# Two of three additions in each sum of features: from GpSimd instructions to accumulating transfers

## The chip, the core and the metric

The kernel runs on one core of a Trainium2 chip. The metric is the device time of one execution in microseconds; smaller is better. A core has TensorE (PE in the profile) for matrix products, VectorE (DVE), ScalarE (ACT) and GpSimd (POOL) for elementwise work, and SyncE (SP), which here issues the transfers. Sixteen DMA engines carry out transfers for all of them.

## What is computed

The reference is a mixture of eight gated experts plus one shared expert, all of them applied to every token, added to the input:

```
g = einsum('bsd,edf->ebsf', h, Wg)
u = einsum('bsd,edf->ebsf', h, Wu)
expert_outs = einsum('ebsf,efd->ebsd', silu(g) * u, Wd)
expert_output = einsum('be,ebsd->bsd', gating_probs, expert_outs)
shared = einsum('bsf,fd->bsd', silu(h @ Sg) * (h @ Su), Sd)
return x + (1 - sg) * expert_output + sg * shared
```

`x` has 8 batch rows of 512 tokens with 256 channels, in 32-bit floats. There are 8 experts with 1024 hidden features each, and the shared one is treated as a ninth.

## The kernel before, in words

**Tiling.** The work is cut into 36 units: 2 halves of the batch (4 batch rows each), 9 experts, and 2 groups of 512 hidden features. In a unit there are four slices of 128 hidden features, numbered by i, and four batch rows, numbered by j. The unit needs the 16 products of slice i with batch row j, once for the gate (m = 0) and once for the up projection (m = 1), then 16 tiles of features h[i,j] = silu(gate) x up x gating weight (`finish`, L449 to L460; 128 features by 512 tokens each, 256 KB), and then their product with the down weights, summed over slices and experts.

**Fewer products.** The products are not all made directly. The four diagonal ones (i = j) are made from the two halves of the 256 channels (`P_step` L463, `Q_step` L487), and the twelve others come in six pairs (`PAIRS`, L65: (1,0), (0,2), (3,0), (1,2), (3,1), (3,2)) from sums and differences of inputs and of weights, with three matmuls for each pair and m (`R1_step` L508, `R_step` L518). Tiles named v, b are such forms of the inputs, loaded by SP; u, wb, at are forms of the weights, made by GpSimd (L380 to L406) with some help of ScalarE (L402). The down projection uses the same device (`down`, L562): besides three matmuls per pair with forms ud, wd of the down weights (`d_forms`, L427) it needs, for each slice n, the row sum rows[n] = h[n,0] + h[n,1] + h[n,2] + h[n,3] over the four batch rows, and for each batch row n the column sum cols[n] over the four slices.

**The sums.** Each of the eight sums of a unit takes three additions, 24 in all. After the last feature tile of a pair is made, `h_sums` (L530) appends four entries to the list `u.sums`: for pair (i,j) a row and a column addition of h[i,j], then a row and a column addition of h[j,i]. `add_sum` (L542) takes the list's first entry and issues its addition on GpSimd (L548). The first addition of a sum opens a tile (pool `sum`, 8 buffers) and writes h[n,n] plus the other feature tile into it; the second and third add one more feature tile to it in place. So over the list, the entries numbered from 1, the sums come in this order: rows 1, cols 0, rows 0, cols 1, rows 0, cols 2, rows 2, cols 0, rows 3, cols 0, rows 0, cols 3, rows 1, cols 2, rows 2, cols 1, rows 3, cols 1, rows 1, cols 3, rows 3, cols 2, rows 2, cols 3. In the last unit only the first three pairs are treated so (12 additions).

**The order of the work.** TensorE's and GpSimd's instruction orders are written by hand (`HAND`, L833; ScalarE's too in the first unit): each engine runs its instructions in program order, and waits on other engines where data are needed. The strings `HUB`, `BLOCK`, `ORDER`, `FIRST`, `LAST` (L808 to L814) interleave steps G of a unit's gate and up products (`gate_up`, L734) with steps D of the down projection of the unit before (`down`). The sums of a unit are issued beside steps G: one at every second step once the unit's own steps are past 22 (`TAKE`), and the rest at each step of the next unit until step 22 (L881 to L887). `down` reads the sums after pairs 0 to 4 in the order p0, q0, pair 5, q1, p1, q2, p2, q3, p3 (L644), where "p n" is the matmul with rows[n] (in `carried`, L596, shown as b<-rows,wd at L591) and "q n" that with cols[n] (in `single`, L604, shown as q<-cols,ad or q<-cols,wd at L607). Before each of them `flush_sums` (L550) issues what additions of that sum are still in the list.

**Buffers around it.** Feature tiles h rotate through 11 buffers (L80), sums through 8 (L81), b and wb through 2 each (L77), v through 3 (L76). A buffer is written again only after all its readers are done; the framework puts in the waits. SP issues the loads of v (L300), b (L317), w (L364) and wd (L411) in program order as their buffers come free. Before the change GpSimd issues no transfers.

Of the kernel before, what the change touches and what calls it, by code (L numbers as in the profile page):

```python
# [11 lines left out]
ALU = mybir.AluOpType  # L12
# [4 lines left out]
def kernel(  # L17
# [79 lines left out]
    gp = nc.gpsimd  # L97
# [246 lines left out]
    for h in range(NH):  # L344
        for e in range(NE):
            for g in range(GRP):
                u = Unit()
# [194 lines left out]
    def add_sum(u):  # L542
        which, n, at = u.sums.pop(0)
        sums = getattr(u, which)
        first = n not in sums
        if first:
            sums[n] = sumpool.tile([P, S], F32, tag="sum", name=f"{which}{n}_{u.name}")
        gp.tensor_tensor(sums[n], u.h_[n, n] if first else sums[n], u.h_[at], ALU.add)  # L548

    def flush_sums(u, which, n):  # L550
        while any(w == which and k == n for w, k, _ in u.sums):
            add_sum(u)
# [304 lines left out]
    for u in units:  # L857
# [6 lines left out]
        for what in FIRST if u.n == 0 else LAST if nxt is None else ORDER:  # L864
            if what == "G":
# [15 lines left out]
                if nG > TAKE and nG % 2 == 0 or nxt is None:  # L881
                    for _ in range(2 if nxt is None else 1):
                        if u.sums:
                            add_sum(u)
                for _ in range(2 if u.n and units[u.n - 1].opens else 1):
                    if nG < TAKE and u.n and units[u.n - 1].sums:
                        add_sum(units[u.n - 1])  # L887
# [69 lines left out]
```

## Time and profile before

| What | Value |
|---|---|
| Runs | 2445.86, 2445.99, 2448.1 us (median 2445.99) |
| Profiled execution, first to last instruction (span) | 2444.9 us, 22752 instructions |
| What lies around the span | 1.1 us to the runs' median; the page gives no other time for the execution |
| One unit of work | 66.95 us |
| Matmul of 128x512, start to start | 0.43 us |
| Addition of a sum on GpSimd, median | 1.27 us |
| DMA, mean share of the 16 engines, queue of SP | 34.3% |
| Granted TensorE clock | 1.00 |

How to read the profile: "busy" lines give each engine's busy time, its share of the span, and its instruction count. The "chain" follows the work that ended last backwards, from each instruction to what released it. A group line has source line, engine, operation, output<-inputs, shapes and count, then total busy time and mean time of one in ns, then idle time of the engine before such instructions, with what ended most of it. A timeline line has start, duration, engine, source line, operation, names and count, and in brackets the idle time before it and its releaser. A window line has the stretch, its length, the busy time of PE, weight loads, DVE, ACT and POOL, then the clock, the DMA share and GB/s. A DMA issue line ends with KB each and the median time from issue to landing in us.

### The profile page before, as it was taken

The numbers are of one execution on the slowest core, as the hardware profiler recorded it, in microseconds if no ns is written. First come the engines' busy times: TensorE is split into PE (matmuls) and PEld (weight loads), VectorE is DVE, ScalarE is ACT, GpSimd is POOL, SyncE is SP. The second block draws the span as 40 slices with busy tenths as digits, with TensorE's granted clock in tenths as the row PEclk, the third lists the DMA queues.
The fourth block names the chain that finished last, engine by engine and source line by source line (L and its number), as shares of the span: only waits on it lengthen the run. The fifth ranks groups of instructions, "written<-read, shape, count | busy, mean of one in ns | idle before, by whom it ended". The sixth has DMA issues, their size and how long they took to land.

```text
span 2444.9 us, 22752 instructions
## 1 busy us (share of the span) xinstructions
PE 2431.5 (99%) x5722; PEld 1079.6 (44%) x5722; DVE 1937.4 (79%) x2889; ACT 1247.2 (51%) x2308; POOL 2095.8 (86%) x2335
## 2 busy tenths in 40 slices
PE   9999999999999999999999999999999999999998
PEld 4444444444444444444444444444444444444444
DVE  7777878777777777787997777777877777777787
ACT  4555554554555555545455555555455455555543
POOL 7988888898988989898888888888888888888883
PEclk9999999999999999999999999999999999999999
DMA  4333333343333333344353222322333333232322
GB/s 160 99 104 112 101 113 114 103 134 100 128 108 97 106 111 95 106 131 126 112 138 119 92 84 90 96 84 88 100 103 103 104 95 95 84 95 89 95 91 82
DMA packets 219793, 255.82 MB, mean 105 GB/s; under 512 B 63632, under 2 KB 156048, under 8 KB 219664
## 3 DMA queue, kind: packets, MB, share of 16 engines
q1 hardware_dynamic: 219376, 254.34, 34.3%
q8 instruction: 48, 0.79, 0.1%
q14 instruction: 81, 0.66, 0.1%
q10 hardware_dynamic: 288, 0.04, 0.0%
HBM read 238.59 MB, written 15.73 MB: 104 GB/s over the span
## 4 chain that ended last, share of the span: by engine, by line
PE 96%; DVE 1%; POOL 1%; DMA 0%; issue 0%; ACT 0%; SPq 0%; DVEq 0%; ACTq 0%; POOLq 0%
PE c L521 30%; PE c L511 15%; PE c L489 10%; PE c L466 10%; PE r L607 7%; PE r L630 7%; PE S L591 5%; PE b L591 5%; PE q L607 5%; PE s L607 2%; PE tail L715 0%; DVE h L457 0%; POOL wd L437 0%; DMA sgt<-ondB_sharedgateprob_dram 0%; DVE accb L582 0%
## 5 line engine op out<-in xcount | busy, mean ns | idle before, releaser
L521 PE MATMUL c<-b,wb 128*128 128x512 f32 x1728 | 847.5, 592 | 0.0
L452 ACT ACTIVATE sg<-c 128x512 f32<-128x512 f32 x576 | 343.8, 597 | 587.2 <-DVE c L526 343.6
L457 DVE SCALAR_TENSOR_TENSOR h<-sg,coef,c 128x512 f32<-128x512 f32 x576 | 427.8, 743 | 235.1 <-PE c L521 132.4
L521 PEld LDWEIGHTS c<-b,wb 128*128 128x128 f32 x1728 | 327.9, 190 | 412.4 <-issue 389.8
L511 PE MATMUL c<-v,u 128*128 128x512 f32 x864 | 441.6, 593 | 1.2 <-ACT c L506 1.2
L548 POOL TENSOR_TENSOR rows<-rows,h 128x512 f32<-128x512 f32 x282 | 372.4, 1321 | 0.0
L548 POOL TENSOR_TENSOR cols<-cols,h 128x512 f32<-128x512 f32 x282 | 361.0, 1280 | 0.0
L516 DVE TENSOR_TENSOR c<-D,c 128x512 f32<-128x512 f32 x432 | 298.9, 692 | 77.8 <-ACT sg L452 57.9
L526 DVE TENSOR_TENSOR c<-c,D 128x512 f32<-128x512 f32 x432 | 298.6, 691 | 18.7 <-PE c L521 18.5
L466 PE MATMUL c<-x,w 128*128 128x512 f32 x572 | 274.5, 592 | 0.0
L404 POOL TENSOR_TENSOR wb<-u,wb 128x256 f32<-128x256 f32 x108 | 79.0, 732 | 222.4 <-ACT wb L402 222.4
L511 PEld LDWEIGHTS c<-v,u 128*128 128x128 f32 x864 | 163.4, 190 | 209.2 <-issue 167.4
L607 PE MATMUL r<-h,wd 128*128 128x512 f32 x426 | 217.5, 592 | 0.0
L630 PE MATMUL r<-X,ud 128*128 128x512 f32 x426 | 217.5, 592 | 0.0
L537 DVE TENSOR_TENSOR X<-h,h 128x512 f32<-128x512 f32 x213 | 208.4, 978 | 6.9
L489 PE MATMUL c<-x,at 128*128 128x512 f32 x432 | 209.6, 593 | 2.4 <-DVE P L482 2.2
L499 ACT COPY D<-c 128x512 f32<-128x512 f32 x284 | 165.9, 584 | 86.8 <-DVE h L457 86.8
L548 POOL TENSOR_TENSOR rows<-h,h 128x512 f32<-128x512 f32 x144 | 199.5, 1385 | 0.0
L548 POOL TENSOR_TENSOR cols<-h,h 128x512 f32<-128x512 f32 x144 | 186.4, 1294 | 0.0
L472 ACT COPY P<-c 128x512 f32<-128x512 f32 x216 | 126.6, 587 | 107.0 <-PE c L466 102.5
L466 PEld LDWEIGHTS c<-x,w 128*128 128x128 f32 x572 | 108.5, 190 | 135.8 <-issue 111.4
L590 ACT COPY S<-accS 128x512 f32<-128x512 f32 x135 | 79.6, 590 | 152.7 <-DVE accV L578 144.9
(110 smaller groups left out, 3478.4 us busy)
## 6 DMA issues: line engine op xcount, KB each, us to landing
b<-xs SPq DMA_DIRECT2D x210, 512.0 KB, 3.6
v<-xs SPq DMA_DIRECT2D x210, 256.0 KB, 2.6
w<-in_L_cond_Wg_dram SPq DMA_DIRECT2D x128, 128.0 KB, 3.4
w<-in_L_cond_Wu_dram SPq DMA_DIRECT2D x128, 128.0 KB, 3.5
wd<-in_L_cond_Wd_dram SPq DMA_DIRECT2D x32, 512.0 KB, 5.0
f<-xd SPq DMA_DIRECT2D x12, 512.0 KB, 3.3
xs<-f SPq DMA_DIRECT2D x18, 256.0 KB, 3.0
xin<-in_x_dram SPq DMA_DIRECT2D x16, 256.0 KB, 4.0
```

The lines of the kernel that those rows point to most:

```text
L452: nc.scalar.activation(s, bank, AF.Silu)
L457: ve.scalar_tensor_tensor(t, u.sg[i, j], coef[:, u.e, b : b + 1], bank, ALU.mult, ALU.mult)
L466: nc.tensor.matmul(bank, u.raw[i][:, m, 0], xhub[u.h, i][:, 0], start=True, stop=True)
L489: nc.tensor.matmul(bank, u.at[i][:, m], xhub[u.h, i][:, 1], start=False, stop=True, skip_group_check=True,)
L511: nc.tensor.matmul(bank, u.U[p][:, m], u.V[p], start=False, stop=True, skip_group_check=True)
L516: ve.tensor_sub(other, u.Ds[j, m], bank)
L521: nc.tensor.matmul(bank, u.W[p][:, r, m], u.VB[p][:, r], start=False, stop=True, skip_group_check=True,)
L526: ve.tensor_add(bank, bank, u.Ds[j, m])
L548: gp.tensor_tensor(sums[n], u.h_[n, n] if first else sums[n], u.h_[at], ALU.add)
L591: nc.tensor.matmul(po, w, b, start=not full, stop=True, skip_group_check=full)
L607: nc.tensor.matmul(po, w, b, start=True, stop=True)
L630: nc.tensor.matmul(A, u.Ud[p], u.X[p], start=False, stop=True, skip_group_check=True)
```

## The change

In `add_sum` the first addition of a sum stays a GpSimd instruction. The second and third become transfers that GpSimd issues, with the feature tile as source and the sum tile as destination, and with an accumulate: each element that arrives is added to what is there. List, order, tiles and buffers are the same.

```diff
         first = n not in sums
         if first:
             sums[n] = sumpool.tile([P, S], F32, tag="sum", name=f"{which}{n}_{u.name}")
-        gp.tensor_tensor(sums[n], u.h_[n, n] if first else sums[n], u.h_[at], ALU.add)
+        if first:
+            gp.tensor_tensor(sums[n], u.h_[n, n], u.h_[at], ALU.add)
+        else:
+            gp.dma_start(sums[n], u.h_[at], accum_op=ALU.add)
```

## The prediction

> **What bounds the kernel now.** I read the engines' busy shares first, then the chain that ended last.
>
> ```profile
> PE 2431.5 (99%) x5722; PEld 1079.6 (44%) x5722; DVE 1937.4 (79%) x2889; ACT 1247.2 (51%) x2308; POOL 2095.8 (86%) x2335
> ...
> PE 96%; DVE 1%; POOL 1%; DMA 0%; issue 0%; ACT 0%; SPq 0%; DVEq 0%; ACTq 0%; POOLq 0%
> ```
>
> TensorE sets the end: it holds 96% of the chain. A busy share is an average, so I then asked for busy time by stretch, with PE's first.
>
> ```profile
> 100.00:1200.00 1100.00, 1099.40 (x2561) 485.81 (x2560) 873.46 (x1300) 566.50 (x1048) 967.05 (x1069) 1.00 0.37 112
> 1200.00:2350.00 1150.00, 1148.50 (x2676) 507.66 (x2675) 913.94 (x1360) 592.20 (x1095) 989.48 (x1097) 1.00 0.33 98
> ```
>
> From 100 to 2350 us TensorE is idle for 0.6 + 1.5 = 2.1 us, at clock 1.00. Matmuls of 512 columns follow each other every 0.43 us. So a lighter GpSimd has 2.1 us to give back there. The remaining idle time, some 11 us, is before 60 us, where the first addition has only just run (42.1 us), and after 2370 us, where the timeline lays PE's gaps to ScalarE copies and VectorE accumulations. The change can hardly gain; the question is whether it makes TensorE wait.
>
> Next, what is changed: the groups of line 548.
>
> ```profile
> L548 POOL TENSOR_TENSOR rows<-rows,h 128x512 f32<-128x512 f32 x282 | 372.4, 1321 | 0.0
> L548 POOL TENSOR_TENSOR cols<-cols,h 128x512 f32<-128x512 f32 x282 | 361.0, 1280 | 0.0
> ```
>
> These 564 instructions (733 us) become transfers. The 288 first additions, the groups rows<-h,h and cols<-h,h, stay.
>
> Last, when the sums are needed. One unit of work takes 66.95 us. GpSimd's timeline of one of them, on both sides of its last wait for another engine:
>
> ```profile
> 1350.01 0.73 POOL L404 TENSOR_TENSOR wb<-u,w 128x256 f32<-128x256 f32 x1 [0.47 <-PE c L521]
> ...
> 1354.19 1.27 POOL L548 TENSOR_TENSOR cols<-cols,h 128x512 f32<-128x512 f32 x1
> ...
> 1357.78 1.27 POOL L548 TENSOR_TENSOR rows<-rows,h 128x512 f32<-128x512 f32 x1
> ...
> 1360.23 1.27 POOL L548 TENSOR_TENSOR cols<-cols,h 128x512 f32<-128x512 f32 x1
> 1361.45 1.28 POOL L548 TENSOR_TENSOR rows<-rows,h 128x512 f32<-128x512 f32 x1
> ...
> 1363.91 1.28 POOL L548 TENSOR_TENSOR cols<-cols,h 128x512 f32<-128x512 f32 x1
> 1365.13 1.28 POOL L548 TENSOR_TENSOR rows<-rows,h 128x512 f32<-128x512 f32 x1
> ...
> 1367.59 1.27 POOL L548 TENSOR_TENSOR cols<-cols,h 128x512 f32<-128x512 f32 x1
> 1368.83 1.27 POOL L548 TENSOR_TENSOR rows<-rows,h 128x512 f32<-128x512 f32 x1
> ```
>
> And TensorE's, the readers of the sums:
>
> ```profile
> 1365.15 1.02 PE L607 MATMUL q<-cols,ad 128*128 128x512 f32 x2
> ...
> 1370.30 1.02 PE L607 MATMUL q<-cols,ad 128*128 128x512 f32 x2
> ...
> 1372.88 1.02 PE L591 MATMUL b<-rows,wd 128*128 128x512 f32 x2
> ```
>
> GpSimd's 24 additions per unit run in the order of the list `u.sums`, so I can number them. Number 22, at 1367.59, completes cols[2]; its reader starts at 1370.30. Done at 1368.86, it has 1.44 us to spare (number 23, for rows[2], 2.78; number 18, for cols[1], 3.66). Over the whole trace the spare time of number 22 is 1.4 us in nearly every unit, and 0.6 in three. **This is the narrow place.**
>
> [...] The trace of before has no transfer on GpSimd's queue[...]. [...] The trace's plain transfers of the same 256 KB:
>
> ```profile
> v<-xs SPq DMA_DIRECT2D x210, 256.0 KB, 2.6
> ...
> xd<-xt SPq DMA_DIRECT2D x8, 256.0 KB, 2.5
> ```
>
> [...]
>
> **The change, part by part.** *Removed:* 16 of 24 additions a unit, 16 x 1.3 = 20.8 us of GpSimd. *Added:* 16 transfers, each holding GpSimd for a time c[...], and landing L later. Both are unknown. For c, the low end is SP's 0.34 us per issue of v[...]; I take 1.2[...]. For L, 2.6 - 0.34 = 2.3 for the plain load after its issue[...]: 2.9. Low end 2.0[...], high end 4.0[...]. Neither can be below nothing: a landing follows its issue.
>
> *Deadline of number 22.* It starts six changed additions (16 to 21) after the wait at 1350.01, which is tied to TensorE and does not move. At 1.25 us from start to start now, it starts 6 x (1.25 - c) earlier; it has 2.71 us from 1367.59 to 1370.30 and needs c + L. TensorE's stall per unit is
> c + L - 2.71 - 6 x (1.25 - c) = 7c + L - 10.21.
> With 1.2 and 2.9: 8.4 + 2.9 - 10.21 = **1.1 us**. The matmul is in TensorE's in-order queue, so all later matmuls shift, and the next unit repeats it: nothing catches up, as PE has no idle time. It doesn't add up within a unit, since number 23's and 24's deadlines move with the stall. 34 units have this order (the last differs, and the next to last has 2.5 us to spare): 34 x 1.1 = 37, and 3 x 0.8 = 2 more for the three narrower ones: **39 us**.
>
> *Other deadlines, same c and L.* Number 18: 4.92 us from its start to its reader, plus 2 x 0.05 gained, against 4.1: holds by 0.9. Number 19, 5.0 to spare before: holds.
>
> *New waits on GpSimd's own queue.* A third addition must wait until the second transfer into the same tile has landed, and holds everything behind it on GpSimd: ud and wd forms, later u and wb. The closest pair, 16 and 18, starts 6.0 us apart and needs 4.1; 20 and 24 start 7.4 apart. No wait, and if L were 5, still none for the first pair below c = 1. The second addition waits for a GpSimd addition that ended long before.
>
> *Feature buffers.* h tiles are now held until a transfer has read them, up to 3 us longer. Eleven buffers for 16 tiles a unit come round after 11/16 x 66.95 = 46 us; the last reader starts 20 us after the tile is made (made 1351.4, read 1371.3). Cost nothing; if that cover went, VectorE's line 457 would wait. That line already shows 69.5 us of waits put down to rows L548, but they end together with the matmul of line 521 that it needs too, at the same 7.73 us spacing as neighbours put down to PE: no tightness.
>
> *Queues passed.* SP's loads keep their order[...]. b lands 3.6 us after issue and is read some 9 us after: doubled, it still holds. What GpSimd frees (0.05 x 16 = 0.8 us a unit) goes into its waits for ACT wb and PE c. Nothing.
>
> Sum against the profiled execution: 2444.9 + 39 = 2484; the runs' median is 1.1 above its span, so **2485 us**.
>
> **Rivals.**
> - *Hidden (not slower).* The stall vanishes when 7c + L is at most 10.2: at L = 2.9, c below 1.04; at L = 2.4, below 1.11. For it: [...]each tenth saved on c counts seven times. [...] Time: 2446, and at most 2 us less, since PE has no more idle time.
> - *GpSimd itself becomes late.* Above c = 1.25 the five transfers (10, 11, 13, 14, 15) between its wait for wb near 1335 and that at 1350.01 also run late, by 5 x (c - 1.25) less the 0.47 us idle there. At c = 1.6: 3.9 + 1.3 = 5.2 us a unit, 34 x 5.2 = 177: about 2625. [...] Against: nothing in the trace but the absence of the operation.
> - *Faster:* needs 5 us of idle PE time to be reached; only the ends of the kernel hold that much, and the additions aren't in the way there.
>
> **Numbers.** Landing late at cols[2], GpSimd not behind (2451 to 2550): 0.45. GpSimd late (above 2550): 0.17. Hidden (2441 to 2451): 0.34. Faster beyond that: 0.04. About 0.2% (5 us) is what a measurement can tell from no change; so faster 0.04, same 0.34, slower 0.62. Range 2444 to 2600: below lie the faster case and the lower edge of the hidden one (0.1 together), above the higher half of the late case (0.1).
>
> **What the profile after would show.** Right: PE line 607, q<-cols, waits about once a unit, by about a microsecond, for a transfer into cols; PE busy time unchanged with the span longer; GpSimd's transfers 1.1 to 1.3 us apart where they follow each other. If its waits are several microseconds, or GpSimd runs without its wait for ACT wb, the late case. If cols[2] lands before its reader, hidden. Wrong altogether: waits of line 457 for h buffers, b or v loads landing late, or a third addition that blocks GpSimd until the second lands.

## The result and the profile after

| | Before | After |
|---|---|---|
| Median of the runs | 2446.76 us (the three runs above and one of 2447.54 us) | 2466.51 us (2463.04 to 2467.86, four runs) |
| Profiled execution: own time, span | span 2444.9 us | 2463.04 us, span 2461.3 us |

The ratio is 1.008, interval 1.0067 to 1.0092: the kernel became slower by 19.8 us, where I had forecast 39. The profiled execution is the fastest of the four, and its span is 16.4 us longer than before.

The page of the kernel after, from its top to its DMA issues (a group's last columns are busy time and mean ns, then idle before; a DMA issue ends with the median us to landing):

```profile
PE 2436.0 (99%) x5722; PEld 1079.7 (44%) x5722; DVE 1955.2 (79%) x2889; ACT 1246.6 (51%) x2308; POOL 1885.6 (77%) x2335
...
q0 software_dynamic: 81216, 147.89, 34.3%
...
PE 92%; DVE 3%; POOL 2%; DMA 2%; issue 1%; ACT 0%; SPq 0%; DVEq 0%; ACTq 0%; POOLq 0%
...
L551 POOL DMA_DIRECT2D rows<-h x282 | 342.5, 1264 | 1.8 <-DVE h L457 1.8
...
rows<-h POOLq DMA_DIRECT2D x282, 256.0 KB, 4.2
cols<-h POOLq DMA_DIRECT2D x282, 256.0 KB, 3.7
```

TensorE's share of the chain fell from 96% to 92%; VectorE, GpSimd, the transfers and "issue" share what it lost. GpSimd is 210 us less busy. VectorE, whose instructions the change doesn't touch, is 17.8 us busier. That is the odd line. By stretch:

```profile
100.00:1200.00 1100.00, 1096.32 (x2553) 484.21 (x2552) 874.00 (x1290) 565.31 (x1045) 865.19 (x1062) 1.00 0.73 173
1200.00:2350.00 1150.00, 1146.75 (x2669) 505.94 (x2668) 917.96 (x1358) 592.01 (x1096) 884.73 (x1093) 1.00 0.69 160
```

TensorE is idle for 3.7 + 3.3 = 7.0 us here, before 2.1. So 4.9 us of the 16.4 were lost in the 2250 us of steady work, and 11.5 before 100 us and after 2350. A stall of 1.1 us in each of 34 units would have put nearly all of it inside. The additions and TensorE's reader in an ordinary unit:

```profile
1436.69 0.88 POOL L551 DMA_DIRECT2D cols<-h  x1
1437.28 1.18 POOL L551 DMA_DIRECT2D rows<-h  x1
1437.84 1.11 POOL L432 TENSOR_TENSOR ud<-wd,ad 128x128 f32<-128x128 f32 x1
1439.03 0.73 POOL L437 TENSOR_TENSOR wd<-ud,wd 128x256 f32<-128x256 f32 x1
...
1442.68 0.86 POOL L551 DMA_DIRECT2D cols<-h  x1
```

```profile
1447.46 1.02 PE L610 MATMUL q<-cols,ad 128*128 128x512 f32 x2
```

Number 22 of the list starts at 1442.68, 4.78 us ahead of its reader (2.71 before the change):

```profile
L551 POOL DMA_DIRECT2D cols<-h x1: 862/862/862, 1442.7 to 1442.7; - x1
...
DMA to landing us min/median/max: 3.3/3.3/3.3
```

This one transfer lands 3.3 us after its start (the median of all transfers into cols is 3.7). It has 1.5 us to spare, and the matmul shows no wait. TensorE's line 610 waits for cols twice in the whole trace, 3.2 us together. The steady unit still takes 66.95 us.

The time went to a few places instead. The time between the starts of TensorE's matmuls beyond 0.43 us, less the same in the same place before, is: 3.8 us at 59 us, 1.5 at 733, 2.1 at 1174, 0.7 at 1284, 1.4 at 1308, 2.8 at 2410. The clock was granted at half after 2409.3 for 6.8 us (matmuls start 0.86 us apart there, not 0.43; 3.1 us lost), and for 3.4 us after 47.2 (about 0.5 in the gap ahead of it and 1.6 at half clock), where no transfer has run yet: the first starts at 50.6. That makes 17.5; the rest, -1.1, is gaps of before that are shorter after. Those at 1174 and 1308 are the two waits for cols. The others are of another kind. VectorE and GpSimd at 727 us:

```profile
726.48 0.74 DVE L457 SCALAR_TENSOR_TENSOR h<-sg,coef,c 128x512 f32<-128x512 f32 x1
727.25 4.32 DVE L537 TENSOR_TENSOR X<-h,h 128x512 f32<-128x512 f32 x1
731.49 0.68 DVE L516 TENSOR_TENSOR c<-D,c 128x512 f32<-128x512 f32 x1
```

```profile
724.39 0.86 POOL L551 DMA_DIRECT2D rows<-h  x1
725.01 1.00 POOL L404 TENSOR_TENSOR wb<-u,w 128x256 f32<-128x256 f32 x1
725.71 0.98 POOL L405 TENSOR_TENSOR wb<-w,u 128x256 f32<-128x256 f32 x1
726.39 1.52 POOL L275 TENSOR_TENSOR f<-f,f 128x512 f32<-128x512 f32 x1
...
729.52 1.49 POOL L549 TENSOR_TENSOR rows<-h,h 128x512 f32<-128x512 f32 x1
730.73 1.12 POOL L551 DMA_DIRECT2D cols<-h  x1
735.61 0.72 POOL L404 TENSOR_TENSOR wb<-u,wb 128x256 f32<-128x256 f32 x1 [3.77 <-ACT wb L402]
```

X = h - h of line 537 takes 4.32 us; before the change no instance took over 1.6 (min, median and max in ns):

```profile
L537 DVE TENSOR_TENSOR X<-h,h x213: 681/1035/1599, 36.6 to 2402.2; 128x512 f32<-128x512 f32 x107
```

After the transfer at 724.39 (number 5) each GpSimd instruction ends about 0.3 us after the next has started: 725.01 + 1.00 is past 725.71, and so on until GpSimd runs out of work at 731.8. X ends ahead of that, at 731.57, which is 0.56 us after the last GpSimd addition (729.52 + 1.49 = 731.01). Three more VectorE instructions with two inputs in SBUF are stretched so: line 310 (b<-v,x) at 52.2 by some 5 us (5.72), X at 1277.4 (3.37) and at 2404.1 (3.96). They too end 0.56 us after the last GpSimd addition. Three of the four lie in the run of GpSimd work that follows number 5; the one at 1277.4 follows number 8, at 1276.7. All lie in places where this run has no pause: the first unit, the preparation of inputs (lines 271 to 277), the start of the second half, the last unit. In the ordinary unit above, the overlap ends where an instruction reads what the one before it wrote: ud ends at 1437.84 + 1.11 = 1438.95, and wd, which reads it, starts after that, at 1439.03. The big TensorE gaps follow these four.

### The profile page after: what moved, and what is told of

Read it like the earlier page. It is cut to its first block, busy times and chain, and to the rows that moved or that the text cites. A ratio compares the mean times of both kernels' runs of the same rounds, so it can differ in the third digit from the quotient of the medians.

```text
span 2461.3 us, 23416 instructions
## 1 busy us (share of the span) xinstructions
PE 2436.0 (99%) x5722; PEld 1079.7 (44%) x5722; DVE 1955.2 (79%) x2889; ACT 1246.6 (51%) x2308; POOL 1885.6 (77%) x2335
## 3 DMA queue, kind: packets, MB, share of 16 engines
q0 software_dynamic: 81216, 147.89, 34.3%
## 4 chain that ended last, share of the span: by engine, by line
PE 92%; DVE 3%; POOL 2%; DMA 2%; issue 1%; ACT 0%; SPq 0%; DVEq 0%; ACTq 0%; POOLq 0%
PE c L521 28%; PE c L511 14%; PE c L489 9%; PE c L466 9%; PE r L610 7%; PE r L633 7%; PE S L594 5%; PE b L594 5%; PE q L610 5%; PE s L610 2%; DMA w<-in_L_cond_Wu_dram 1%; DMA cols<-h 1%; DVE h L457 1%; PE tail L718 0%; DVE X L537 0%
## 5 line engine op out<-in xcount | busy, mean ns | idle before, releaser
L457 DVE SCALAR_TENSOR_TENSOR h<-sg,coef,c 128x512 f32<-128x512 f32 x576 | 427.1, 741 | 229.1 <-PE c L521 204.5
L404 POOL TENSOR_TENSOR wb<-u,wb 128x256 f32<-128x256 f32 x108 | 79.2, 733 | 353.1 <-ACT wb L402 353.1
L551 POOL DMA_DIRECT2D rows<-h x282 | 342.5, 1264 | 1.8 <-DVE h L457 1.8
L551 POOL DMA_DIRECT2D cols<-h x282 | 285.5, 1015 | 7.3 <-issue 4.4
L537 DVE TENSOR_TENSOR X<-h,h 128x512 f32<-128x512 f32 x213 | 227.9, 1070 | 6.9
L549 POOL TENSOR_TENSOR cols<-h,h 128x512 f32<-128x512 f32 x144 | 209.9, 1458 | 0.0
L404 POOL TENSOR_TENSOR wb<-u,w 128x256 f32<-128x256 f32 x108 | 88.2, 817 | 123.3 <-PE c L521 119.9
```

The costliest lines, as they stand in the source:

```text
L457: ve.scalar_tensor_tensor(t, u.sg[i, j], coef[:, u.e, b : b + 1], bank, ALU.mult, ALU.mult)
L549: gp.tensor_tensor(sums[n], u.h_[n, n], u.h_[at], ALU.add)
L551: gp.dma_start(sums[n], u.h_[at], accum_op=ALU.add)
```

## The experiments

After these readings I held the theory that the loss is mainly these **hold-ups** of VectorE (A in the expectations): without a transfer, an instruction with two inputs in SBUF is let in between two GpSimd instructions (X took at most 1.60 us before the change), and after a transfer it waits until GpSimd runs out of work (4.32 us at 727). A smaller part would be the third additions that land late. The rivals put all of it on late landings, or on the added DMA traffic. Medians are compared with runs of the kernel before on the same chip, 2446.59, 2447.15 and 2446.82 us in the three groups of runs.

**1. Number 5 alone back on GpSimd.**

```diff
+        elif which == "rows" and at == (0, 2):
+            gp.tensor_tensor(sums[n], sums[n], u.h_[at], ALU.add)
```

> Edit: number 5 of each unit's list (the second addition of rows 0) is a GpSimd addition again; the other transfers stay (529). Theory A (VectorE is held up: after a transfer GpSimd's instructions overlap, and a VectorE instruction with two inputs in SBUF that comes in such a run waits until GpSimd pauses): in the changed kernel the long VectorE instructions at 52, 727, 1277 and 2404 us (3.4 to 5.7 us) all begin in the run of instructions that follows number 5, so all four go, and with them the waits of TensorE at 59, 733, 1284 and 2410 us and the half clock at the end: about 2450 us. Theory B (landings too late at the readers, as forecast): nothing but one transfer fewer per unit, none of them ahead of the late readers at 1174 and 1308 us: 2465 us. Theory C (the added DMA traffic slows other loads): 35 of 564 transfers fewer, 2465 us.

Measured: 2454.2 us, ratio 1.0028 (1.0018 to 1.0039). 528 transfers stay. One of 16 transfers a unit makes up 12 of the 20 us. The longest X is 2.15 us, at 1274.9, after number 8, which is still a transfer; line 310 takes at most 2.71. What stays is mostly a late q at 1169.8 (2.47 us) with half clock after it. For A, and against traffic, which fell only from 34.3 to 32.2% of the engines' time.

**2. Only the second additions as transfers.**

```diff
+        elif k == 3:
+            gp.tensor_tensor(sums[n], sums[n], u.h_[at], ALU.add)
```

(k counts the additions of a sum.)

> Edit: only the second addition of each sum is a transfer (282), the third is a GpSimd addition again. Theory A: number 5 is a second addition, so the hold-ups stay: slower than before by 8 to 14 us, about 2457. Theory B: the readers get GpSimd's own additions as the last, late landings at readers vanish, and GpSimd waits at most for a second transfer to land: about 2447 if all of the loss was there, 2463 if only the 3.7 us of the two late readers was.

Measured: 2462.2 us, ratio 1.0063 (1.005 to 1.0075). The time is nearer to the rival's figure than to mine, so alone it doesn't decide. The trace does: TensorE has no wait for rows or cols left, the traffic is halved (16.7%), and the hold-ups are all there: line 310 takes 7.12 us at 51.1, X 4.27, 3.91 and 3.97 at 729.6, 1277.7 and 2406.0. Half clock follows three of the gaps. The hold-ups can cost over 15 us by themselves; I had put them too low.

**3. Only the third additions as transfers** (k == 2 in the edit above).

> Edit: only the third addition of each sum is a transfer (282), the second is a GpSimd addition again. Theory A: no transfer lies ahead of the held-up VectorE instructions, so about 2447 to 2450 us. Theory B: the landing latency stands at every reader, and five of the six additions ahead of the critical one give GpSimd less time back (three of six are second additions: 0.34 us each is lost to the lead, 1.0 us in all, as against 1.1 us to spare), so between 2447 and 2465, with short waits at cols 2.

Measured: 2449.45 us, ratio 1.0012 (1.0005 to 1.0019). Number 5, a second addition, is a GpSimd instruction here. The time is within what I gave for either theory, so it doesn't decide. Against what I expected of A, four X are still held up, for 2.6 us (three) and 4.38 us (at 1278.5), all behind the third additions 10 and 11, so number 5 isn't the only transfer that does it; no large gap lies behind them. In three units q waits for a transfer, 0.8 us together.

**4. Operations by themselves.** A kernel of its own that computes nothing of the reference: VectorE subtracts, with both inputs in SBUF, while GpSimd works. Phase T: twelve additions. M: two additions, a transfer, nine additions. N: as M with a second transfer. D: eight transfers.

> The operations by themselves; computes nothing of the reference. GpSimd runs 12 additions of 128x512 back to back (phase T), the same with one accumulating transfer after the second addition (phase M), with two (phase N), and 8 accumulating transfers alone (phase D), while VectorE runs 12 subtractions with two inputs in SBUF; each phase waits for the one before, twice over. Theory A: in T no subtraction is longer than about one GpSimd addition more than its own 0.7 us (under 2 us); in M and N one after the transfer lasts until GpSimd's run ends, several us (4 to 10); in D none is held up for long[...]. Rival[...]: in M and N at most about 1 us more near the transfer, and the worst hold-ups in D.

Lines of phases T and M:

```profile
L54 DVE TENSOR_TENSOR subT<-readyT,a x24: 692/1744/1750, 5.7 to 106.1; 128x512 f32<-128x512 f32 x24
```

```profile
L54 DVE TENSOR_TENSOR subM<-readyM,a x24: 675/677/12037, 28.0 to 131.1; 128x512 f32<-128x512 f32 x24
```

Without a transfer, the two engines take turns: 1.74 us each time. With one, a subtraction of 0.68 us lasts 12.04 us, to the end of GpSimd's nine additions. In N, it lasts 11.61 us, across the second transfer. In D, beside eight transfers and no addition, none is over 0.69. So it isn't the transfer that holds VectorE up, but GpSimd additions that follow it. Eight transfers take 0.89 us of GpSimd each, from the first's start to the last's end.

**5. The whole change, and after numbers 5 and 8 a dependent pair of tiny GpSimd additions**, the second of which reads what the first wrote.

```diff
+            if at in ((0, 2), (2, 0)):
+                one = const.tile([P, 2], F32, tag="one", name="one")
+                gp.tensor_tensor(one[:, 0:1], ident[:, 0:1], ident[:, 0:1], ALU.add)
+                gp.tensor_tensor(one[:, 1:2], one[:, 0:1], ident[:, 0:1], ALU.add)
```

> Edit: all 564 transfers stay, but numbers 5 and 8 of each unit's list are each followed by two GpSimd additions of 128x1, the second of which needs the first's result[...]. Theory A (GpSimd's instructions overlap after a transfer, and that holds VectorE up): the pair ends the overlap, the hold-ups of 3 to 6 us on lines 537 and 310 vanish, and what stays is the 2 to 4 us of late readers where the halves of the batch change: about 2450 us. If it is [...]the transfer's traffic, that holds VectorE up, nothing changes: 2465 us.

Measured: 2454.74 us, ratio 1.0029 (1.0019 to 1.004). The tile X in this kernel, then in the kernel after:

```profile
L537 DVE TENSOR_TENSOR X<-h,h x213: 678/1090/1699, 37.3 to 2409.6; 128x512 f32<-128x512 f32 x107
```

```profile
L537 DVE TENSOR_TENSOR X<-h,h x213: 676/1066/4320, 35.4 to 2417.9; 128x512 f32<-128x512 f32 x107
```

All transfers stay, the traffic stays (35.5%), and the hold-ups are gone: the longest X is down from 4.32 to 1.70 us, line 310's from 5.72 to 1.78. It is some 5 us slower than I expected. What is left are late landings: b waits for rows for 2.42 us at 1289.2, with half clock after it, and there are shorter gaps at q at 1167, 1310 and 2315. These gaps and the half clock add up to nearly all of the 7.6 us.

**6. Each addition as two transfers of half the columns.** This doubles what GpSimd spends on them.

```diff
-            gp.dma_start(sums[n], u.h_[at], accum_op=ALU.add)
+            for k in range(2):
+                at_k = ts(k, S // 2)
+                gp.dma_start(sums[n][:, at_k], u.h_[at][:, at_k], accum_op=ALU.add)
```

> Edit: each second and third addition is made by two accumulating transfers of 128x256 instead of one of 128x512 (1128 transfers of 128 KB). The forecast's deadline of number 22 is tested with a larger c: one transfer now holds GpSimd 0.9 us. If that goes by the count of rows (128 again), c is 1.8 per addition and TensorE waits 1.8 + 2.6 - 2.71 + 6 x 0.55 = 5.0 us a unit at cols 2, and up to 7.3 with the lateness gathered before: 2446 + 34 x (5.0 to 7.3), 2615 to 2695 us. If it goes by bytes, c stays near 0.9 and the time near 2466.

Measured: 2765.5 us, ratio 1.1301 (1.1285 to 1.1316), 318 us slower. TensorE's wait (us in total, times, longest):

```profile
PE q L612 <- DMA cols<-h: 208.4, 68, 7.4
```

It waits twice a unit, for 1.48 us at one q and 4.12 at the next in the unit at 1550 us. GpSimd now spends 1.77 us per addition, twice 0.89, though the bytes are the same. The mean granted clock is 0.963, so the clock is at half for 2 x 0.037 x 2767 = some 205 us; TensorE is busy for 164 of these, which costs 82. With the 208 this is 290 of the 318. It is 70 us more than the upper end I gave, since I hadn't counted the half clock. The rival that I forecast in the prediction is real; the change just doesn't reach it.

**7. The whole change with number 22 pushed back** by five idle GpSimd additions of 128x128 (`idle` is a spare tile).

```diff
+            if which == "cols" and at == (3, 2):
+                for _ in range(5):
+                    gp.tensor_tensor(idle, ident, ident, ALU.add)
```

> Edit: five GpSimd additions of 128x128 into a spare tile ahead of number 22 (the last of cols 2) in every unit; their result is not used. They take 0.42 to 0.54 us each from start to start, 2.1 to 2.7 in all. If the deadline stands as the changed kernel's timeline shows it (starts 1442.68, landing 3.7 later, reader at 1447.46: 1.1 us to spare), TensorE waits 1.0 to 1.6 us at q<-cols in each of 34 units: 34 to 54 us more, 2500 to 2520 us. If landings have more to spare than that, 2466.

Measured: 2506.02 us, ratio 1.0238 (1.0222 to 1.0254), as expected: 39.5 us over the changed kernel.

```profile
PE q L614 <- DMA cols<-h: 25.6, 29, 3.8
```

The five take 2.25 us from start to start. With 1.5 us to spare (4.78 - 3.3) the stall should be about 0.8 us a unit. A unit takes 67.89 us (median) instead of 66.95, 0.94 more, which is 32 us in 34 units. The other 7 or so are single longer waits, the longest of 3.8 us, and more half clock (mean 0.996 against 0.998). The median landing of 3.7 us would give 1.17 a unit and 40 us in all, but that agreement is chance. So the formula of the prediction holds within some 0.2 us a unit, and so does its claim that nothing catches up.

**8. Which VectorE instruction, and what ends it.** Again a kernel that computes nothing of the reference. M as before; W: M with the dependent pair after the transfer; U: M with a one-input VectorE instruction; E: two transfers, then additions.

> The operations by themselves; computes nothing of the reference. Phase M: two GpSimd additions, one accumulating transfer, nine additions, beside 12 VectorE subtractions with two inputs in SBUF. W: the same, with the dependent pair of 128x1 additions right after the transfer. U: as M, but VectorE's instructions have one input. E: two transfers first, then nine additions. Theory A: M has one subtraction of some 12 us again; W none over 2 to 3 us; U none over 1 us; E has one that lasts from the first addition to the end of the run, some 10 us. [...]

```profile
L61 DVE TENSOR_TENSOR subW<-readyW,a x24: 677/1744/1751, 28.9 to 127.8; 128x512 f32<-128x512 f32 x24
```

```profile
L59 DVE TENSOR_SCALAR subU<-readyU x24: 411/412/11912, 50.5 to 152.6; 128x512 f32<-128x512 f32 x24
```

W: the pair brings back the turns of 1.74 us of phase T. M and E: at most 12.03 and 11.94 us. U was a miss: I expected an instruction with one input not to be held up, and it was, for 11.9 us instead of 0.41. It isn't the number of inputs alone that decides.

**9. Only the second additions as transfers (run 2), with the pair (run 5).**

> Edit: only the second additions are transfers (282), and numbers 5 and 8 are followed by the dependent pair of 128x1 GpSimd additions. If the loss of the changed kernel has two parts, the hold-ups of VectorE after number 5 (with the half clock that follows some) and the late landings of third additions at their readers, both are gone here: 2447 to 2449 us, no VectorE instruction of lines 537 and 310 over 3 us and no wait of q or b for a transfer. If there is a third part that goes with the count of transfers (traffic), it stays, half as large: 2450 us or more.

Measured: 2447.67 us, ratio 1.0005 (0.9997 to 1.0013): no difference from the kernel before that can be measured, as expected. With the hold-ups cured (one X of 2.77 us stays, at 68.0) and no third addition to land late, no loss is left that can be told from noise, though 282 accumulating transfers remain (17.2% of the engines' time). One thing I hadn't expected: at 1304.2 a q waits for 1.4 us, for a third addition that GpSimd makes late, since it had waited 2.7 us at 1294.7 for a second transfer to land. By the interval, a loss of up to some 3 us could still hide here. Nor is anything gained: GpSimd is far lighter, and TensorE has no idle time to give back. No version here beats the kernel before.

**10. Plain transfers in place of accumulating ones.** The second and third additions are left out: each overwrites the sum.

```diff
-            gp.dma_start(sums[n], u.h_[at], accum_op=ALU.add)
+            gp.dma_start(sums[n], u.h_[at])
```

> Edit: the 564 transfers copy instead of accumulating, so the second and third additions are left out; order, waits and sizes are the same. [...]the plain transfer holds GpSimd 0.7 us instead of 0.9 and lands 3.1 to 3.6 us after its issue instead of 3.7 to 4.2, and its DMA share is about two thirds. The hold-ups of VectorE should remain in about the same places, since they follow any transfer that GpSimd issues: 2455 to 2465 us. [...]

Measured: 2453.28 us, ratio 1.0027 (1.0017 to 1.0038), a little below my range. The holding time, the landing and the DMA share too came out lower than I had expected; what I expected of these three was an estimate that no run had shown. The group and the page's queue line:

```profile
L551 POOL DMA_DIRECT2D cols<-h x282: 538/562/571, 59.1 to 2407.5; - x141
```

```profile
q0 software_dynamic: 45120, 147.89, 15.6%
```

A plain transfer holds GpSimd for 0.56 us, lands in cols after a median of 2.3 us (3.7 accumulating) and takes 15.6% of the DMA engines (34.3%). No reader is late. The hold-ups stay, X up to 4.11 us and line 310 up to 2.42: they come with a transfer from GpSimd, not with its accumulate. The later ends are gone: after the transfer at 721.70, instructions of 0.73 us take 0.74 us, and X is held up behind them all the same, for 4.11 us at 724.5. So the 0.3 us is no necessary sign of a hold-up.

## Why the prediction was right in sign and wrong in its mechanism

The direction and the range held, but that was luck: the likeliest case, a stall in every unit that gave 2485 us, did not happen. The right sign and half of the size came mainly from effects that no case of mine named. Landing late at cols, the forecast's own effect, occurs in two places, once at cols[2] (number 22, 1174 us) and once at cols[1] (number 18, 1308 us).

- **"TensorE sets the end; the change can hardly gain": right.** Run 9 shows the best case, 1.0005.
- **"Deadline of number 22": the step that failed, by the size of c.** I took c = 1.2 us; in the trace two transfers and the ud form after them take 2.34 us from start to start (1436.69 to 1439.03), less 0.54 for a form with no transfer ahead of it: 0.90 each. So number 22 starts 6 x (1.25 - 0.90) = 2.1 us earlier, not 0.3. L was also too high, but matters less: 3.3 - 0.9 = 2.4 for this number 22 (2.8 by the median of 3.7), against 2.9. The formula gives 7 x 0.90 + 2.4 - 10.21 = -1.5, not +1.1: hidden. With this L and my c it would still give +0.6. c was the term counted seven times, and I had written that below 1.04 the stall vanishes. My c, and what L has beyond the 2.3 us of a plain load, were estimates that the trace of before, with no transfer on GpSimd's queue, doesn't show. Run 10 measures a c of 0.56 for a plain transfer, and the accumulate takes 0.34 more.
- **The rival "hidden" therefore named the steady state rightly**, but its time, 2446, missed by 20 us, since it asked only about this one deadline.
- **"Other deadlines" hold with landings of 3.7 us; they don't with late ones.** In two places cols landed 6.8 and 7.5 us after the start. The first of them, and its stretch:

```profile
1173.94 1.10 PE L610 MATMUL q<-cols,ad 128*128 128x512 f32 x2 [1.96 <-DMA cols<-h]
```

```profile
1167.00:1174.00 7.00, 5.04 (x13) 1.99 (x11) 5.33 (x9) 3.68 (x7) 5.39 (x9) 1.00 1.05 236
...
1440.00:1450.00 10.00, 10.00 (x24) 4.37 (x23) 8.45 (x13) 5.08 (x10) 9.61 (x15) 1.00 0.93 176
```

  The DMA share is over 1 there (1.05, and 1.09 at 1300 to 1308); the stretch of the ordinary unit has 0.93. Ahead of the first place, SP loads the inputs of the other half of the batch in 512 KB pieces, beside the unit's own loads; ahead of the second, it issues twelve loads within 14 us, which had come behind the storing of results. In the first place the transfers themselves start as far apart as in the ordinary unit. That SP's loads make the landings late is argued from these windows; no run took them away. My range for L ended at 4.0, an estimate made with the mean shares of before in mind (0.37 and 0.33); I didn't ask where the share was already high.
- **"New waits on GpSimd's own queue: no wait": nearly right.** Three third additions wait, 3.0 us in all, two of them in the places of the late landings. GpSimd has time for it.
- **"Feature buffers: nothing": right.** Line 457's idle time went from 235.1 to 229.1 us.
- **"Queues passed": right.** The transfers take 34.3% of the engines' time. v lands after 3.0 us (2.6), b after 3.7 (3.6), and TensorE hardly waits for them (0.2 us). What GpSimd frees went into its wait for ACT wb: 222.4 us before, 353.1 after, as written.
- **"GpSimd itself becomes late": didn't happen.** It needs c above 1.25. Run 6, at 1.77, shows what TensorE then does.
- **What no step asked: how long other engines' instructions take beside the new operation.** The trace of before already had X at up to 1.60 us, against 0.68 at least, and in phase T the two engines take turns (1.74 us). After a transfer, VectorE waits for the whole run of GpSimd instructions, 12.0 us for nine, and that no view of before shows. Why the transfer does this isn't shown. In the kernel after, GpSimd's instructions behind it end about 0.3 us past the next one's start, and the overlap ends where one reads what the one before it wrote; the pair, which is such a case, ends the hold-ups (1.75 us at most in phase W). But in run 10 the hold-ups come without those later ends (X at 4.11 us). No run looks inside GpSimd, so the cause there is open.
- **Half clock.** After some gaps the clock is granted at half for 3.4 us or a multiple of it. In each trace all half stretches begin on one grid of 3.41 us (in the kernel after at 47.25 and 2409.27 us, 692 pieces apart). So it matters how a gap lies on this grid. The 3.5 us at 2410 fill most of one piece, the 3.8 us at 59 are split over two (TensorE's busy time comes first after the length):

```profile
2405.86:2409.27 3.41, 0.75 (x2) 0.00 (x0) 3.41 (x4) 0.00 (x0) 2.48 (x3) 1.00 0.61 134
54.07:57.49 3.42, 1.55 (x4) 0.38 (x2) 3.42 (x1) 0.00 (x0) 3.42 (x5) 1.00 0.26 77
57.49:60.90 3.41, 1.66 (x4) 0.87 (x5) 3.03 (x6) 1.60 (x3) 0.70 (x1) 1.00 0.68 189
```

  TensorE is busy for 22% of the first piece, and half clock follows; for 45 and 49% of the others, and none does. In eight of the traces (the kernel after and runs 1, 2, 5, 6, 7, 9 and 10, without their first 30 and last 12 us), 50 pieces at full clock are followed by half clock, and in 49 of them TensorE is busy for 41% or less; the 5628 followed by full clock have 44% or more. The one that doesn't fit ends at 47.2 (51%), so that one is open. Half clock makes up some 30% of the loss (3.1 + 1.6 of 16.4 us here, 82 of 318 in run 6).

The shares are not fully additive. Hold-ups alone cost 15.6 us (run 2), late landings with all transfers 7.6 (run 5), and together they are 23 against 19.8 measured; both figures include half clock, which depends on where a gap falls. In run 9, without either kind, no loss can be told from noise; a third part of up to some 3 us isn't excluded. With only the third additions moved the loss is 2.9 us (run 3), of which 0.8 are waits of q for a transfer.

## What to carry to other kernels

Before an operation is moved from an engine to a queue, price the term that is counted most often by a measurement, not by an estimate; here 0.3 us on c decided the sign of the stall. Ask then what the new instruction does to the instructions of the engines that work beside it, and look at the longest instance of each group, not at its mean: four of some 2900 VectorE instructions cost over half of the loss. And lay a deadline not only against the mean DMA share, but also against the stretches in which it is highest: both late landings lie in such stretches.

## What the hardware showed that I had not expected

- GpSimd additions after a transfer that GpSimd issued hold up a VectorE instruction with two inputs in SBUF until the last of them ends: 12.0 us in phase M, against 1.74 without the transfer (phase T). In the kernel after, all four held-up instructions end 0.56 us after the last GpSimd addition. Plain transfers do it too (X up to 4.11 us in run 10). Two tiny GpSimd additions, one reading what the other wrote, end it (1.75 at most in phase W).
- A VectorE instruction with one input, normally 0.41 us, is held up as well (11.9 us in phase U).
- An accumulating transfer of 256 KB within SBUF holds GpSimd for 0.90 us, of which 0.3 shows only as later ends of the instructions behind it; a plain one holds it for 0.56. Half the columns cost as much as all (1.77 for two).
- An accumulate takes 2.2 times the DMA engines' time of a plain transfer of the same bytes (34.3 against 15.6%) and lands some 1.4 us later (3.7 against 2.3 for cols).
- In the eight traces counted above, half clock came after a piece of the 3.41 us grid in which TensorE was busy for 41% or less in 49 of 50 cases. The length of a gap alone doesn't tell: the one of 3.8 us at 59, split over two pieces (45 and 49%), drew none.
